# Four images on one core: when the second layer's rows T and the next image's second rows xx are loaded

## The chip, the core and the metric

The kernel runs on one core of one Trainium2 chip. The metric is the device time of one execution in microseconds; several executions are made and the median is given. One execution is also taken with the hardware profiler, and every duration of a single instruction comes from that one.

## What is computed

The input x has 4 images of 32 channels and 128 x 128 points. In layer 0 each image is rearranged into 128 rows (32 channels by 2 x 2 points) of 4096 columns:

```python
q = xs.reshape(B, C * R * R, hw)
energy = jnp.einsum('bci,bcj->bij', q, q)      # 4096 x 4096
d = jnp.sqrt(jnp.diagonal(energy, axis1=1, axis2=2))
attn = jax.nn.softmax(energy / (d[:, :, None] * d[:, None, :]), axis=-1)
out = gamma * jnp.einsum('bcj,bij->bci', q, attn) + xs
```

Layer 1 takes the result as 4096 tokens of 128 numbers an image:

```python
t = t + _L1_attn_ref(_ln_t(t), Wk, Wq, Wv)      # linear attention, 8 heads
t = t + _L1_ffn_ref(_ln_t(t), router_w, router_b, expert_w, expert_b)   # 2 of 8 experts
```

## The kernel before

**Layer 0, `attend`.** The 4096 columns of an image are 8 chunks of 512. Row i of the work goes over the chunks jc = 0 to i; so a row has i blocks off the diagonal and one on it, and the last row, i = 7, is the longest. For each quarter of a block PE makes the energies (pe, L556), ACT their exponentials (pr, L559), and PE multiplies them into the row's sum (po, L440). The energies are symmetric. Each block off the diagonal is therefore used a second time, transposed: DVE transposes it in pieces of 32 x 32 into F (L369); SP writes F to DRAM, 1 MB (blocks, L483, in `move`); when that has landed SP brings it back in another order by four DMAs of 256 KB (G, L491, in `bring`); and 57 units of the planned clock later PE multiplies G into the sum of the other chunk (pg, L375). Diagonal blocks go the same way in smaller form (L498, L506, L396). Three buffers are there for F and three for G.

**Layer 1.** `layer1` makes all that comes after layer 0 for an image. Its `all_parts` is the steady stream: it starts near the end of the image's own `attend` and runs on beside the next image's. T holds the image's rows, 2 MB in SBUF in a single buffer (tag "T" of `big1`); `input_rows` loads it from x by 4 groups of 4 DMAs of 128 KB (image 0: 8 groups with half as much each; the DMAs are those of L279, tile T). `close_rows` adds the result of layer 0 to T and normalises it, `attention_rows` adds the attention, stores T to DRAM (t2, L897) and normalises it a second time, and `sorted_experts` handles the experts. It scatters the normalised rows into DRAM sorted by expert (POOL, L989), SP loads the sorted rows (L1013), PE multiplies them (pys), SP stores the results (ys, L1035), POOL gathers two rows for each token (yb, L1114), DVE combines them into acc, which ACT's queue has fetched from t2 (L1090), and SP puts acc into the output (L1096, `put`). The tokens are handled in two halves. Image 3 has nobody beside it, and its experts are worked out without sorting in `last_parts`.

**`prep`.** `prep(b, kc, st)` loads a quarter of image b's rows (xx, 4 DMAs of 128 KB, also L279), transposes them on PE (ptq, L313), sums their squares on DVE, takes the power -1/2 on POOL (L164), scales, and transposes again (ptn, L346). Of the next image the quarters 0 and 1 are made during the current one, 2 and 3 at the beginning of its own.

**The order.** The order of every engine's instructions is written out by hand; each engine and each DMA queue takes its own in that order. A clock counts work of PE, and t is the percent of an image that is done. Each stream of instructions is a generator. The streams in `timed` have a begin, an end and a count of steps: such a stream moves a step whenever t has passed its share of the stretch. T and xx are such streams. The steady stream moves a step every 10 units of the clock. So a DMA's place in SP's queue is set by t, and what is issued before it on SP goes first. In images 1 to 3, by this plan, the last normalisation that reads the previous image's T is issued at t = 32.1; its scatters at 34.4 to 60; the loads of sorted rows at 50.5 to 79; the gathers at 71 to 95; the puts from 79 on; the first `close_rows` of the image at 94.

The places the change touches are the planner's lines L1327 to L1332.

Of the kernel before, what the change touches and what calls it, by code (L numbers as in the profile page):

```python
# [22 lines left out]
def kernel(  # L23
# [45 lines left out]
    B, C, H, W = x.shape  # L69
# [66 lines left out]
    def setup_sorting():  # L136
        def iota(dst, pattern, part=0):
            nc.gpsimd.iota(
                dst, pattern=pattern, base=0, channel_multiplier=part, allow_small_or_imprecise_dtypes=True
            )  # L140

        iota(rank_below, [[1, P]], part=-1)
        nc.vector.tensor_scalar(rank_below, rank_below, 0.0, None, ALU.is_gt)
        iota(upto, [[1, E], [-1, E]])
        nc.vector.tensor_scalar(upto, upto, 0.0, None, ALU.is_ge)
        iota(tiles_of[:, 0, :], [[P, HR]])
        iota(tile_no[:, :, 0], [[1, NT]])
        yield
        yield

        rows = x.rearrange("b c h w -> (b c h) w")
        step = NT * P // 8
        for g in range(16):
            inst = nc.scalar.dma_start(xs[g // 8][ts(g % 8, step), :], rows[ts(g, step), :])
            xs_made[g // 8].append(inst.ins)
            yield
            yield
# [5 lines left out]
    def pow_neg_half(dst, src):  # L163
        pinned(nc.gpsimd.tensor_tensor(dst, src, neg_half.to_broadcast(list(src.shape)), ALU.pow))  # L164
# [13 lines left out]
    def idle(n):  # L178
        for _ in range(2 * n):
            yield  # L180

    def keep_running(n, pool=None, tag=None):

        bank = psum_t("spare") if pool is None else pool.tile([P, CH], F32, tag=tag, name="spare")
        for _ in range(n):
            nc.tensor.transpose(bank[:, :P], ident, ident)
# [4 lines left out]
    def hold(name, evict, alloc=psum_t):  # L191


        while len(held) >= banks[0]:
            held[0]()
        bank = alloc(name)

        def done():
            if done in held:
                held.remove(done)  # L200
                evict(bank)

        held.append(done)
        return bank, done
# [69 lines left out]
    def load_tokens(dst, b, k0, nk, queues=(nc.sync, nc.sync)):  # L274
        src = tokens(x, b)
        for s in range(2):
            for r1 in range(2):
                p0 = s * 64 + r1 * 32
                queues[r1].dma_start(dst[p0 : p0 + 32], src[s, r1, :, k0 : k0 + nk, :])  # L279


    def prep(b, kc, st):

        if b == 0:
            if kc == 0:
                st["all"] = big1.tile([P, 4, 8, HW2, 2], F32, tag="T", name="xx_0")
            xx = st["all"][:, kc]
        else:
            xx = xin.tile([P, 8, HW2, 2], F32, tag="xx", name=f"xx_{b}_{kc}")
        first = b == 0 and kc == 0  # L290
        load_tokens(
            xx.rearrange("p k w r -> p k (w r)"), b, 8 * kc, 8, (nc.sync, nc.scalar if first else nc.sync)
        )
        qT = qpool.tile([P, 2, NJ, P], F32, tag="qT", name=f"qT_{b}_{kc}")
        st.setdefault("qT", {})[2 * kc] = qT[:, 0]
        st["qT"][2 * kc + 1] = qT[:, 1]
        yield
        yield
        yield from idle(2 if b else 1)

        def load_half(g, pt):
            nc.vector.tensor_copy(
                qT[:, :, 2 * g : 2 * g + 2, :].rearrange("p s j (r c) -> p (j r) s c", c=64),
                pt.rearrange("p (m s c) -> p m s c", s=2, c=64),
            )

        for g in range(2):
            yield
            pt, done = hold(f"ptq_{b}_{kc}_{g}", partial(load_half, g))
            for jj in range(2):  # L310
                for r2 in range(2):
                    k = 4 * g + 2 * jj
                    nc.tensor.transpose(  # L313
                        pt[:, ts(2 * jj + r2, P)], xx[:, k : k + 2, :, r2].rearrange("p k w -> p (k w)"), ident
                    )
            yield
            done()
        yield
        yield
        ss = stat.tile([P, 2 * NJ], F32, tag="ss", name=f"ss_{b}_{kc}")  # L320
        rn = stat.tile([P, 2 * NJ, 1], F32, tag="rn", name=f"rn_{b}_{kc}")
        for s in range(2):
            sq = work.tile([P, NJ, P], F32, tag="qs", name=f"sq_{b}_{kc}_{s}", bufs=2)
            nc.vector.tensor_tensor(sq, qT[:, s], qT[:, s], ALU.mult)
            nc.vector.tensor_reduce(ss[:, ts(s, NJ)], sq, AX.X, ALU.add)  # L325
            if first:
                pow_neg_half(rn[:, ts(s, NJ), 0], ss[:, ts(s, NJ)])
            elif s == 1:
                pow_neg_half(rn[:, :, 0], ss)
            yield  # L330
            yield
        yield from idle(1)
        if first:
            keep_running(22, ps_g, "pg")
        scaled = []
        for s in range(2):
            qs = work.tile([P, NJ, P], F32, tag="qs", name=f"qs_{b}_{kc}_{s}", bufs=2)
            nc.vector.tensor_tensor(qs, qT[:, s], rn[:, ts(s, NJ)].to_broadcast([P, NJ, P]), ALU.mult)
            scaled.append(qs)
        for s, qs in enumerate(scaled):  # L340
            yield
            qn = npool.tile([P, CH], F32, tag="qn", name=f"qn_{b}_{2 * kc + s}")
            st.setdefault("qn", {})[2 * kc + s] = qn
            pt, done = hold(f"ptn_{b}_{kc}_{s}", lambda p, qn=qn: nc.scalar.activation(qn, p, AF.Copy))  # L344
            for j in range(NJ):
                nc.tensor.transpose(pt[:, ts(j, P)], qs[:, j, :], ident)  # L346
            yield
            done()
        yield
        yield  # L350
# [242 lines left out]
    def input_rows(b, st):  # L593
        st["T"] = T = big1.tile([P, KT, D], F32, tag="T", name=f"T_{b}")
        nk = 4 if b == 0 else 8
        for k in range(0, KT, nk):
            load_tokens(T[:, k : k + nk, :], b, k, nk)
            yield
            yield
            yield from idle(1)  # L600
# [718 lines left out]
    timed = [(first, 0, 1, 4)]  # L1319
    for b in range(B):  # L1320

        if b == 0:
            for kc, begin, end in ((1, 0, 5), (2, 6, 20), (3, 25, 45)):
                timed.append((prep(0, kc, states[0]), begin, end, 12))
            timed.append((setup_weights(), 46, 58, 9))
            timed.append((setup_sorting(), 58, 98, 17))
        if b + 1 < B:  # L1327
            nxt = states[b + 1]
            timed.append((prep(b + 1, 0, nxt), 65, 82, 13))
            timed.append((prep(b + 1, 1, nxt), 83, 99, 13))  # L1330
        begin, end, count = (52, 94, 17) if b == 0 else (55, 75, 9) if b == B - 1 else (82, 99, 9)
        timed.append((input_rows(b, states[b]), begin, end, count))  # L1332
        done = [0] * len(timed)
        start = clock[0]
        closing = None
        for half, _ in enumerate(chain(attend(b, states[b]), finish() if b == B - 1 else ())):
            if half % 2 == 0:
                t = 100 * (clock[0] - start) / UNITS
                moved = []
                if closing is None and t > 84:  # L1340
                    closing = layer1(b, states[b])
                    steady.append([closing.first_parts() if b == B - 1 else closing.all_parts(), clock[0]])
                for n, (steps, begin, end, count) in enumerate(timed):
                    if t >= begin and done[n] * (end - begin) < (t - begin) * count:
                        moved.append(steps)
                        done[n] += 1
                for stream in steady:
                    if clock[0] >= stream[1]:
                        stream[1] = clock[0] + PACE
                        moved.append(stream[0])  # L1350
            for steps in moved:
                next(steps, None)
        for steps, *_ in timed:
            for _ in steps:
                pass
        timed = []
        if b + 1 < B:
            timed.append((prep(b + 1, 2, nxt), 2, 20, 13))
            timed.append((prep(b + 1, 3, nxt), 30, 50, 13))
# [43 lines left out]
```

## Time and profile before

| what | us |
|---|---|
| median of three runs | 1753.12 (1751.01 to 1756.18) |
| the profiled execution, whole | 1738.44 |
| its span | 1736.7 |
| PE busy in the span | 1660.1 |
| DVE, ACT, POOL busy | 940.4, 928.7, 513.3 |
| DMA of the hardware queue of SP | 314.91 MB, 64.4% of the 16 engines' span |

The span is the time from the first instruction to the last, and it is a little shorter than the execution. PE busy divided by the span is PE's share. A wait is read from an engine's timeline: the brackets behind an instruction give the idle time before it and what ended it. In the page's DMA row each digit is the busy share of the 16 DMA engines in a fortieth of the span. The granted clock of PE has a mean of 0.988.

### The profile page before, as it was taken

What the parts mean: (1) busy time and instruction counts of PE and PEld (TensorE: products, weight loads), DVE (VectorE), ACT (ScalarE), POOL (GpSimd) and SP (SyncE); (2) the same over time, 40 slices, a digit from 0 to 9 for tenths busy, and PEclk for the clock granted to TensorE, in tenths of its full rate; (3) what the DMA queues carried; (4) which work ended last, traced back from release to release, by engine and by line L of the source; (5) the groups of instructions that cost most, each with busy time, mean ns of one, the idle gap of its engine ahead of it and who ended that gap; (6) DMA issues with size and microseconds to landing.
All of it is one profiled execution on the core that took longest, in us unless ns stands there. A gap on an engine that the chain in (4) does not pass through costs nothing. (4 is left out here: it accounts for less than half of the span.)

```text
span 1736.7 us, 21220 instructions
## 1 busy us (share of the span) xinstructions
PE 1660.1 (96%) x5458; PEld 879.4 (51%) x5458; DVE 940.4 (54%) x2443; ACT 928.7 (53%) x2893; POOL 513.3 (30%) x553
## 2 busy tenths in 40 slices
PE   8999999999999999889999999979999999999887
PEld 5444444455644555445554455534555455544633
DVE  4433334467585335567477334546748533455687
ACT  3555445466565555446565555535556555445376
POOL 1000000011037506540015722552102760464166
PEclk9999999999999999999999999999999999999999
DMA  4675877876567899987567889998656889995001
GB/s 132 199 203 169 213 209 231 249 216 182 178 189 246 254 269 255 254 234 203 163 186 218 251 260 264 259 244 213 200 157 193 244 257 261 272 269 137 1 13 37
DMA packets 240681, 355.25 MB, mean 205 GB/s; under 512 B 27312, under 2 KB 155312, under 8 KB 226480
## 3 DMA queue, kind: packets, MB, share of 16 engines
q1 hardware_dynamic: 220048, 314.91, 64.4%
q0 software_dynamic: 12288, 25.19, 5.0%
q10 hardware_dynamic: 8224, 13.77, 2.9%
q8 instruction: 46, 0.75, 0.2%
q14 instruction: 75, 0.61, 0.1%
HBM read 183.64 MB, written 173.15 MB: 205 GB/s over the span
## 5 line engine op out<-in xcount | busy, mean ns | idle before, releaser
L559 ACT ACTIVATE pr<-pe 128x512 f32<-128x512 f32 (+1 forms) x576 | 322.4, 560 | 544.1 <-PE pe L556 504.7
L440 PE MATMUL po<-pr,qT 128*128 128x512 f32 (+3 forms) x1152 | 552.0, 561 | 3.9 <-ACT o L445 3.9
L375 PE MATMUL pg<-G,qT 128*128 128x512 f32 x880 | 455.5, 599 | 37.0 <-DMA G<-blocks 28.9
L556 PE MATMUL pe<-qn,qn 128*128 128x512 f32 x896 | 463.1, 599 | 1.9 <-ACT pr L559 1.6
L369 DVE STREAM_TRANSPOSE F<-pr 128x512 f32<-128x512 f32 x440 | 306.1, 702 | 150.1 <-ACT pr L559 146.8
L440 PEld LDWEIGHTS po<-pr,qT 128*128 128x128 f32 x1152 | 216.6, 191 | 251.7 <-issue 221.4
L380 ACT ACTIVATE junk<-G 128x512 bf16<-128x512 f32 x440 | 273.0, 620 | 37.6 <-DMA G<-blocks 35.3
L375 PEld LDWEIGHTS pg<-G,qT 128*128 128x128 f32 x880 | 166.9, 192 | 238.1 <-issue 190.1
L1114 POOL DMA_INDIRECT yb<-ys,place x192 | 186.2, 970 | 276.1 <-DMA xn<-xs 102.7
L989 POOL DMA_INDIRECT xs<-xn,place x192 | 185.6, 966 | 118.6 <-ACT pr L559 56.2
L556 PEld LDWEIGHTS pe<-qn,qn 128*128 128x128 f32 x896 | 155.7, 192 | 113.9 <-issue 102.4
L385 DVE TENSOR_TENSOR o<-o,pg 128x512 f32<-128x512 f32 x110 | 75.5, 686 | 212.5 <-PE pg L375 212.0
L164 POOL TENSOR_TENSOR rn<-ss,neg_half 128x8 f32<-128x8 f32 (+1 forms) x17 | 27.7, 1634 | 395.4 <-DVE ss L325 395.4
L559 ACT ACTIVATION_READ_ACCUMULATOR pr<-pe 128x1 f32 x576 | 111.9, 194 | 0.0
L1023 ACT ACTIVATE xn<-pys 128x256 f32<-128x256 f32 (+1 forms) x120 | 44.9, 377 | 104.8 <-PE pys L1056 104.7
L164 POOL TENSOR_TENSOR rsf<-dm_f,neg_half 128x8 f32<-128x8 f32 (+1 forms) x15 | 26.2, 1746 | 235.1 <-DVE sv_f L636 235.1
L1049 PEld LDWEIGHTS pys<-ew_sb,xn 128*128 128x128 f32 x468 | 68.4, 191 | 47.6 <-issue 44.9
L556 PE MATMUL pe<-qn 128*128 128x512 f32 (+3 forms) x256 | 90.7, 437 | 0.7 <-ACT qn L344 0.7
L380 ACT ACTIVATION_READ_ACCUMULATOR junk<-G 128x1 f32 x440 | 84.3, 192 | 0.0
L1032 DVE COPY result<-pys 128x256 f32<-128x256 f32 (+1 forms) x60 | 24.6, 411 | 100.8 <-ACT xn L1023 73.3
L1083 DVE SCALAR_TENSOR_TENSOR acc<-yb,weight,acc 128x128 f32<-128x128 f32 x192 | 65.6, 342 | 21.3 <-DMA yb<-ys,place 13.1
L1049 PE MATMUL pys<-ew_sb,xn 128*128 x468 | 71.2, 275 | 4.1 <-DVE result L1032 4.1
(189 smaller groups left out, 1574.9 us busy)
## 6 DMA issues: line engine op xcount, KB each, us to landing
blocks<-F SPq DMA_DIRECT2D x108, 1024.0 KB
G<-blocks SPq DMA_DIRECT2D x432, 256.0 KB
xn<-xs SPq DMA_DIRECT2D x114, 128.0 KB
below<-F SPq DMA_DIRECT2D x31, 384.0 KB
G<-below SPq DMA_DIRECT2D x124, 96.0 KB
out_dram<-acc SPq DMA_DIRECT2D x128, 64.0 KB
xx<-in_x_dram SPq DMA_DIRECT2D x62, 128.0 KB
ys<-xn SPq DMA_DIRECT2D x60, 128.0 KB
```

The lines of the kernel that those rows point to most:

```text
L164: pinned(nc.gpsimd.tensor_tensor(dst, src, neg_half.to_broadcast(list(src.shape)), ALU.pow))
L369: f()
L375: nc.tensor.matmul(pg.rearrange("p (a f) -> p a f", a=4), st["qT"][i][:, ib, :], G[:, :, ib], start=(ib == 0), stop=(ib == NJ - 1),)
L380: nc.scalar.activation(junk, G[:, :, ib], AF.Copy, accum_out=st["sums"][:, NJ * i + ib, jc : jc + 1])
L385: nc.vector.tensor_tensor(o, o, pg.rearrange("p (a j c) -> p a j c", a=4, c=S), ALU.add)
L440: nc.tensor.matmul(row["po"][:, lo:hi], qT[blk // NJ][:, blk % NJ, :], w, start=start, stop=(row["left"] == 0))
L556: nc.tensor.matmul(pe[:, c0:], qn[jc][:, ts(j, P)], qn[i][:, c0:], start=True, stop=True)
L559: nc.scalar.activation(pr[:, c0:], pe[:, c0:], AF.Exp, accum_out=sums[:, t, i : i + 1]).ins
L989: inst = nc.gpsimd.indirect_dma_start(xs[h], offset(place[:, i, k : k + 1]), xn[:, k, :], None)
L1049: nc.tensor.matmul(p[:, 2 * P + j * D : 2 * P + j * D + D], bufs[4 + g % 2][:, j, :], weights[:, bass.ds(begins[2 * (g % 2) + j], D)], sta ...
L1083: nc.vector.scalar_tensor_tensor(a[:, k % 4, :], yb[k // 4][:, i, k % 4, :], weight[:, i, k, :], a[:, k % 4, :], ALU.mult, ALU.add)
L1114: inst = nc.gpsimd.indirect_dma_start(yb[k // 4][:, i, k % 4, :], None, ys, offset(place[:, i, k : k + 1]))
```

## The change

```diff
         if b + 1 < B:
             nxt = states[b + 1]
             timed.append((prep(b + 1, 0, nxt), 65, 82, 13))
-            timed.append((prep(b + 1, 1, nxt), 83, 99, 13))
-        begin, end, count = (52, 94, 17) if b == 0 else (55, 75, 9) if b == B - 1 else (82, 99, 9)
+            timed.append((prep(b + 1, 1, nxt), 87, 99, 13))
+        begin, end, count = (52, 94, 17) if b == 0 else (36, 47, 9)
         timed.append((input_rows(b, states[b]), begin, end, count))
```

T of images 1 and 2 was planned into 82 to 99 percent of the image and T of image 3 into 55 to 75; all three are now planned into 36 to 47. Image 0's stays at 52 to 94. In images 0, 1 and 2 the second quarter of the next image, `prep(b + 1, 1)`, was planned into 83 to 99 percent and now goes into 87 to 99, with the same number of steps. No instruction is added or removed.

## The prediction

> **What bounds the kernel now.** I read four views of the profile: the page, the busy time by stage (windows), the timeline of PE with what ended its idle time, and the timeline of SP's queue. The page says that TensorE is the bound nearly everywhere and that the DMA engines fill up toward the end of an image.
>
> ```profile
> PE 1660.1 (96%) x5458; PEld 879.4 (51%) x5458; DVE 940.4 (54%) x2443; ACT 928.7 (53%) x2893; POOL 513.3 (30%) x553
> ...
> DMA  4675877876567899987567889998656889995001
> ```
>
> PE is busy 1660.1 of 1736.7 us, so 76.6 us are idle, and only idle or half-clocked PE time can be won. The DMA row rises to 9s three times: near the ends of images 1, 2 and 3. (Counting exponentials of L559, 144 to an image, the images begin at 15, 370, 782 and 1199 us.) The stages around the change:
>
> ```profile
> core 0: us, PE busy (x) PEld busy (x) DVE busy (x) ACT busy (x) POOL busy (x), PEclk, DMA share, GB/s
> ...
> 510.00:545.00 35.00, 34.82 (x100) 17.00 (x99) 25.60 (x70) 17.30 (x55) 24.44 (x26) 1.00 0.75 228
> ...
> 700.00:760.00 60.00, 48.30 (x114) 21.65 (x113) 30.34 (x65) 21.37 (x67) 31.38 (x33) 0.91 0.95 247
> ...
> 1120.00:1200.00 80.00, 65.90 (x177) 31.41 (x176) 46.26 (x112) 32.51 (x101) 35.09 (x35) 0.94 0.95 235
> ...
> 1405.00:1480.00 75.00, 75.00 (x296) 43.63 (x294) 25.86 (x52) 39.72 (x122) 16.51 (x18) 1.00 0.92 248
> ```
>
> Where T is loaded now in images 1 and 2 (700 to 760 and 1120 to 1200), DMA is at 95% and PE loses 11.7 and 14.1 us, at a lowered clock besides. Where T will be loaded (510 to 545 in image 1) DMA is at 75% and PE loses 0.18 us. PE's timeline names what it waits for in the first of the bad stages:
>
> ```profile
> 717.21 2.04 PE L375 MATMUL pg<-G,qT 128*128 128x512 f32 x2 [3.89 <-DMA G<-blocks]
> ...
> 732.16 1.10 PE L375 MATMUL pg<-G,qT 128*128 128x512 f32 x2 [1.85 <-DVE F L369]
> ...
> 748.65 2.05 PE L375 MATMUL pg<-G,qT 128*128 128x512 f32 x2 [5.96 <-DMA G<-blocks]
> ```
>
> The product of a transposed block (pg) needs its four G transfers. G lands late, so SP's queue is the place to look:
>
> ```profile
> 703.11 2.07 SPq L279 DMA_DIRECT2D T<-in_x_dram  x4
> 705.27 0.39 SPq L1035 DMA_DIRECT2D ys<-result  x1
> 705.84 7.41 SPq L491 DMA_DIRECT2D G<-blocks  x4
> 713.29 1.91 SPq L279 DMA_DIRECT2D xx<-in_x_dram  x4
> 715.30 0.39 SPq L483 DMA_DIRECT2D blocks<-F  x1
> 715.79 3.83 SPq L1096 DMA_DIRECT2D out_dram<-acc  x4
> 723.26 1.74 SPq L491 DMA_DIRECT2D G<-blocks  x4
> 725.04 2.55 SPq L279 DMA_DIRECT2D T<-in_x_dram  x4
> 731.65 0.34 SPq L483 DMA_DIRECT2D blocks<-F  x1
> ```
>
> One queue carries everything in program order: the block to DRAM, its return as G, T, xx, the results. G's four issues take 7.41 us instead of 1.74: the trace's semaphore records show eight DMA semaphores used in turn by SP and ACT, and an issue waits until the DMA eight places earlier has landed (the fourth G began at 712.94; the holder, an acc<-t issued on ACT's queue at 706.42, landed at 712.92). So each T group, four DMAs of 128 KB, costs bytes, half of the eight places, and SP's time.
>
> **What the Trainium skill says.** "DMA: Bandwidth & Descriptors", section "Issuing engines are not separate DMA queues": DMAs of all issuing engines share the same 16 DMA engines and interleave; the ACT-issued acc<-t above, 6.5 us under way between SP's transfers, agrees. Same page, "Anatomy of one DMA": waits on semaphores happen on the issuing sequencer, not in the DMA engines; the 7.41 us agree. "TensorE: Matmul & The Clock Gate", section "HAM oscillation": a throttled stretch costs half its length. The trace's clock records have half-clock stretches of 3.41 us from 717.07 and 6.83 us from 747.79, and the pair of L375 took 2.04 us there against 1.10 at 732.16.
>
> **The change, part by part.** Positions are percent of an image's planned clock (UNITS), found by stepping the generators by hand.
>
> (1) T of images 1 and 2 leaves 82.65, 86.22, 90.05 and 93.88 (16 DMAs, 2 MB each image). Price of a group: the DMA packet records give 4096 packets of 512 B at a mean 32 ns over 16 engines, 8.2 us per T, 2.05 per group; the landings of the first group in image 1 lie 0.65 us apart, 2.6. On the queue it is more. From one G to the next in row 7 of image 1 (SP starts 705.84, 723.26, 738.77, 752.04, 767.4, 778.3, 788.4) SP takes 17.4, 15.5, 13.3, 15.4, 10.9, 10.1 us; the 15.5, 13.3 and 15.4 hold a group and a put each, the 10.9 a put alone. A group costs 14.7 - 10.9 = 3.8 us there; the first costs about 2.3. Sum 2.3 + 3 x 3.8 = 13.7 us of queue. Image 2 has 14.8, 15.3, 14.1, 16.3, 11.5, 10.4: the same picture, 4.3 a group.
>
> What PE can win: image 1 idles 3.89 + 1.85 + 5.96 + 1.10 (at 794.8) = 12.8, and runs about 9.4 us at half clock while busy, 4.7: 17.5 in all. Image 2: 2.44 + 3.64 + 5.96 + 2.06 + 0.36 = 14.5, plus 4.4: 18.9. Walking image 1 with the groups gone: G(7,0) lands about 2.5 us earlier (3.89 becomes 1.4), G(7,1) about 7 (its gap closes), G(7,2) about 8 to 9, G(7,3) to G(7,6) 10 to 14. PE without stalls takes about 11 us from pg to pg, as much as the queue then needs. I get 13 us at row 7's end, less part (2).
>
> (2) xx of prep(b+1, 1) moves from 83.42 to 87.24 (image 0) or 87.76 (images 1 and 2), past the issue of a block write and, in images 1 and 2, past G(7,1): 2.6 us of transfer leave in front of one G and stand in front of the next. Its transposes on PE now follow 2.6 to 3.1% behind the load instead of 3.8%: 11 us in place of 15. xx needs 7 us from issue to landing and SP is 5 us behind PE there, so the ptq transposes, queued on PE ahead of everything later, wait. Before, xx landed at 720.1 and PE took it at 722.34, after a stall; that was the whole slack. I take 3 us of wait (bounds 0 and 5) in each of images 0 to 2. In 1 and 2 it partly replaces G(7,2)'s gap; I subtract it whole: 13 - 3 = 10 each. In image 0 it meets the 2.29 us wait for G<-blocks at 339.47, which goes (2.6 us less ahead of it); net +0.5 (bounds -1.5 and +2). The rest of prep is squeezed from 16% to 11% of an image and ends by 98.1 as before; rn of POOL stands behind gathers that end at 95.4. Nothing for it, at worst 1 us.
>
> (3) T of image 3 leaves 55.1 to 68.4. No PE stall lies there (75.00 of 75.00 busy), but the lag it leaves ends in 3.37 us at 1484.58 (pys behind a result buffer whose store is late), then 1.77 and 2.17 for G, and 1.7 of clock: 9.0. DMA stays at 97% to 1560 without T, so I take the first with its clock, 5 us in all (bounds 1 and 9).
>
> (4) T arrives at 36.5, 38.7, 41.6 and 43.9 in all three images. The previous T's last readers are at 32.14 (normalise) and 31.38 (store), 16 us earlier: no wait. Behind the groups on SP stand G(4,2), G(4,3), the diagonal and G(5,0). SP issued G(4,3) until 531.64, it landed at 537.1, PE came at 543.24: 6.1 us to spare, the least of the stage in image 1. Price of a group: below 0.5 if it fills DMA's idle quarter while SP waits for a block to land, 2.6 if not. I take 1.2: three groups 3.6, inside 6.1. Image 3's old groups are the nearest row: four of them at 92% DMA, with no stall. Cover gone, each us over 6.1 is a us of PE. POOL's scatters slow beside them, with nobody waiting before 50.5%.
>
> Sum: image 0 +0.5, images 1 and 2 -10 and -10.5, image 3 -5: **-25 us**. The span goes from 1736.7 to 1711.7; the profiled execution took 1738.44 (1.74 around the span), the median of the runs shown is 1753.12, 14.7 above it. I subtract the same 25 from it: **1728**.
>
> **The rivals.**
> Small gain: the bytes alone count, 2.05 to 2.6 per group up to G(7,2), and the ptq waits and a half-clock stretch stay: -5, -5, -3, about 1740. For it: SP's eight places stay full with puts and blocks. Against: the 10.9 us spacing as soon as no group is in it.
> Large gain: every stall named goes, 17.5 + 18.9 + 9.0 less a few us, about -41: 1712. Against: the ptq wait, and the DMA share of image 3.
> No change: the DMA chain of images 1 and 2 is late already by 700, and xx moved into the worst stretch gives back what T leaves: 1753. Against: 7 to 10 us to spare for G until 657, and 4.2 still at 691.
> Slower: in the new place a group delays the G behind it by p us, as SP waits in order for a block's landing. PE stalls by 3p - 6.1 an image, and 1.7 for the clock. At p = 5 that is 10.6 in each of three images and eats the whole 25 plus 7; it decides from p = 4.2, and at 5.4 the sum is +10, where I put the case: 1763. For it: the queue price of 3.8 in the full stage. Against: a quarter of the DMA time is free.
>
> **How the numbers follow.** Forecast 0.50; small gain 0.20; large gain 0.14; no change 0.07; slower 0.09. A measurement of this kernel tells about 0.3% (5 us) from no change. Faster 0.50 + 0.20 + 0.14 = 0.84, same 0.07, slower 0.09. The range 1708 to 1748 takes in the first three with the bounds of their costs and leaves out the last two, 0.16.
>
> **What would show it.** Right: 700 to 760 with PE near 55 of 60 or more, no 6.83 us half-clock stretch, G-to-G spacing near 11 us in row 7, 510 to 545 at a DMA share over 0.85 with PE still over 34.5 busy, ptq waiting for xx by some us. Wrong: idle at L375 before 570 in image 1, or row 7's spacing still 13 to 15 us with no T in it.

## The result and the profile after

| kernel | median us (lowest to highest) | ratio to before, 95% interval |
|---|---|---|
| before | 1752.07 (1749.98 to 1756.18) | |
| after | 1731.59 (1728.70 to 1733.49) | 0.9881 [0.9853, 0.9909] |

The change saves 20.5 us. The forecast was 1728, so 25. The profiled execution of after took 1730.18 us, with a span of 1728.4.

From the page of after, the engines' busy time and the DMA row:

```profile
PE 1656.8 (96%) x5458; PEld 876.9 (51%) x5458; DVE 939.3 (54%) x2443; ACT 925.8 (54%) x2893; POOL 511.8 (30%) x553
...
DMA  4775778876569899996568979998656988995001
```

PE does the same 5458 instructions. In the DMA row a 9 has come up in the slices 12, 22 and 31 (counted from 0; from 518, 951 and 1339 us), which is T's new place; near the image ends the row stays at 8 and 9. The stages of the prediction, in the windows of after:

```profile
core 0: us, PE busy (x) PEld busy (x) DVE busy (x) ACT busy (x) POOL busy (x), PEclk, DMA share, GB/s
510.00:545.00 35.00, 34.81 (x97) 16.87 (x97) 25.60 (x76) 18.16 (x60) 24.17 (x24) 1.00 0.96 259
700.00:760.00 60.00, 56.26 (x146) 26.37 (x145) 34.03 (x75) 26.14 (x83) 33.98 (x35) 0.94 0.92 256
1120.00:1200.00 80.00, 74.30 (x211) 36.13 (x210) 53.17 (x138) 38.77 (x123) 38.87 (x39) 0.98 0.90 250
1405.00:1480.00 75.00, 73.67 (x291) 43.06 (x292) 28.95 (x59) 40.37 (x125) 15.23 (x16) 1.00 0.88 253
```

In T's new place (510 to 545) the DMA share rose from 0.75 to 0.96, and PE is busy for 34.81 us where it was for 34.82. In the old place (700 to 760) PE went from 48.30 to 56.26 of 60 us. DMA is hardly less busy there (0.95 to 0.92): other transfers moved up. This window favours this profile, in which row 7 begins 8 us later than before (its first G is issued at 713.54, before at 705.84). In the profile of the same kernel from the first group of experiments row 7 begins at 704.57, and the window has

```profile
700.00:760.00 60.00, 53.44 (x135) 24.09 (x134) 38.57 (x91) 24.85 (x78) 35.44 (x36) 0.97 0.97 265
```

against 48.87 busy in before on that chip. PE's timeline of after names what is left of the waits of image 1 (the number in front is the start of the instruction, so a wait lies ahead of it; "issue" means that the profile shows nothing that was waited for):

```profile
583.34 1.22 PE L1049 MATMUL pys<-ew_sb,xn 128*128 x4 [3.74 <-ACT xn L1023]
...
736.38 2.04 PE L375 MATMUL pg<-G,qT 128*128 128x512 f32 x2 [2.70 <-DMA G<-blocks]
...
762.22 1.10 PE L375 MATMUL pg<-G,qT 128*128 128x512 f32 x2 [0.56 <-DMA G<-blocks]
765.58 0.66 PE L346 MATMUL ptn<-ident,qs 128*128 128x128 f32 x4 [2.27 <-issue]
```

The waits at L375 fell from 3.89 + 1.85 + 5.96 + 1.10 to 2.70 + 0.56. Two lines are new. The wait of ptn (2.27 us, prep's second transposes) was not in the prediction. The wait of pys ahead of 583.34 was not either; 3.36 us ahead of 999.91 and 3.44 ahead of 1406.33 are its like in images 2 and 3. The section on the chips below comes back to it. SP's timeline of after through row 7:

```profile
713.54 1.85 SPq L491 DMA_DIRECT2D G<-blocks  x4
...
715.97 10.93 SPq L1096 DMA_DIRECT2D out_dram<-acc  x4
727.06 2.81 SPq L491 DMA_DIRECT2D G<-blocks  x4
...
731.31 2.62 SPq L279 DMA_DIRECT2D xx<-in_x_dram  x4
735.53 4.01 SPq L1096 DMA_DIRECT2D out_dram<-acc  x4
740.39 2.38 SPq L491 DMA_DIRECT2D G<-blocks  x4
...
743.37 10.13 SPq L1096 DMA_DIRECT2D out_dram<-acc  x4
753.67 1.75 SPq L491 DMA_DIRECT2D G<-blocks  x4
```

From one G to the next SP takes 13.5, 13.3, 13.3, 11.1, 11.1 and 9.6 us (before: 17.4, 15.5, 13.3, 15.4, 10.9, 10.1). No T is in the queue now, yet three of the distances are 13 us and not the 11 that was forecast: in two of them a put's four issues take 10.93 and 10.13 us, as those of T's last group did before (10.10 from 755.25); in the third stand xx and a put.

### The profile page after: what moved, and what is told of

Same layout as the page of the kernel before. It is cut to its first block, busy times and chain, and to the rows that moved or that the text cites. A ratio compares the mean times of both kernels' runs of the same rounds, so it can differ in the third digit from the quotient of the medians.

```text
span 1728.4 us, 21211 instructions
## 1 busy us (share of the span) xinstructions
PE 1656.8 (96%) x5458; PEld 876.9 (51%) x5458; DVE 939.3 (54%) x2443; ACT 925.8 (54%) x2893; POOL 511.8 (30%) x553
## 5 line engine op out<-in xcount | busy, mean ns | idle before, releaser
L375 PE MATMUL pg<-G,qT 128*128 128x512 f32 x880 | 453.4, 597 | 14.1 <-DMA G<-blocks 8.7
L375 PEld LDWEIGHTS pg<-G,qT 128*128 128x128 f32 x880 | 167.5, 192 | 214.0 <-issue 187.0
L1023 ACT ACTIVATE xn<-pys 128x256 f32<-128x256 f32 (+1 forms) x120 | 45.0, 377 | 118.3 <-PE pys L1056 67.7
L1049 PEld LDWEIGHTS pys<-ew_sb,xn 128*128 128x128 f32 x468 | 68.5, 192 | 56.3 <-issue 39.0
L164 POOL TENSOR_TENSOR rsa<-dm_a,neg_half 128x8 f32<-128x8 f32 x16 | 26.4, 1650 | 219.3 <-DVE sv_a L636 219.0
L1049 PE MATMUL pys<-ew_sb,xn 128*128 x468 | 72.1, 277 | 11.1 <-ACT xn L1023 11.0
```

The lines of the kernel that those rows point to most:

```text
L375: nc.tensor.matmul(pg.rearrange("p (a f) -> p a f", a=4), st["qT"][i][:, ib, :], G[:, :, ib], start=(ib == 0), stop=(ib == NJ - 1),)
L1023: nc.scalar.activation(bufs[4 + g % 2][:, :n], p[:, : n * P].rearrange("p (j t) -> p j t", t=P), AF.Copy)
L1049: nc.tensor.matmul(p[:, 2 * P + j * D : 2 * P + j * D + D], bufs[4 + g % 2][:, j, :], weights[:, bass.ds(begins[2 * (g % 2) + j], D)], sta ...
```

## The experiments

Twelve runs, in three groups of four; each group ran on one chip, beside runs of before on the same chip (their median is given with the group). Differences in us are those of the medians of one group; between groups the ratios are compared. The diffs are against the changed kernel; where the text says "prep at 83", the line of e1 that puts it there belongs to the edit too and is not shown again.

**First group (before: 1739.80 us).** The change taken apart.

`e1_t_only`: T moved, prep where it was.

```diff
-            timed.append((prep(b + 1, 1, nxt), 87, 99, 13))
+            timed.append((prep(b + 1, 1, nxt), 83, 99, 13))
```

> T of images 1 to 3 moved as in the change, the next image's second rows left at 83. Theory (T's four groups are what makes G late in row 7): at least the whole gain of the change, 20 to 25 us (ratio about 0.987), image 0 unchanged against before, and PE's idle time at L375 in row 7 of images 1 and 2 under half of what it was. Rival (the second rows' shift past G(7,1) is what helps): 10 us or less (ratio 0.995 or above).

Measured: 1711.45 us, 0.9839 [0.9818, 0.9860], 28.4 us saved.

`e2_prep_only`: prep moved, T where it was.

```diff
-        begin, end, count = (52, 94, 17) if b == 0 else (36, 47, 9)
+        begin, end, count = (52, 94, 17) if b == 0 else (55, 75, 9) if b == B - 1 else (82, 99, 9)
```

> Only the next image's second rows moved from 83 to 87, T left in its old places. Theory: no change within 5 us (ratio 0.997 to 1.003), image 0 ends about 2 us later with a wait of ptq for xx. Rival: 10 us faster.

Measured: 1736.82 us, 0.9980 [0.9966, 0.9994].

`e3_after_again` and `e4_before_again`: the two kernels unchanged.

> The change once more, to see whether the three new stalls of about 3.5 us at the first products of the sorted rows (L1049, near 54% of images 1 to 3) belong to the kernel or to one profiled execution. If they belong to it: again three stalls of 3 to 4 us at L1049. If not: fewer, or elsewhere. Time about 0.988 of before.

Measured: 1716.99 us, 0.9871 [0.9851, 0.9891], 22.8 us saved; none of the three waits of pys is in its profile.

> The kernel before once more, since its profiled execution was 14.7 us shorter than the median of its timed ones. Theory: an execution near 1752 us shows the same stalls at L375 in row 7 of images 1 and 2, only longer, by 10 to 15 us in all. Rival: the difference lies elsewhere (a lower clock, the end of the kernel, image 0).

Measured: one execution, 1735.89 us, with much the same waits as the profile of before (35.2 us at L375 against 37.0). It was not an execution near 1752 us, so it does not show where such a one loses its time.

T's move alone is worth more than the whole change: the later prep costs 5.5 us beside it (1716.99 - 1711.45). The profiles show where. PE's groups of instructions in the kernel before on this chip (`e4`; the last columns are the idle time ahead of the group and what ended it):

```profile
L375 PE MATMUL pg<-G,qT 128*128 128x512 f32 x880 | 455.1, 599 | 35.2 <-DMA G<-blocks 30.6 <-DMA out_dram<-acc 1.8 <-DVE acc L1083 1.5
L1049 PE MATMUL pys<-ew_sb,xn 128*128 x468 | 71.6, 276 | 3.7 <-DVE result L1032 3.7
L313 PE MATMUL ptq<-ident,xx 128*128 128x128 f32 x128 | 20.9, 289 | 5.9 <-DMA xx<-in_x_dram 5.9
L346 PE MATMUL ptn<-ident,qs 128*128 128x128 f32 x128 | 19.4, 274 | 0.7 <-DVE qs L338 0.7
```

with T alone moved:

```profile
L375 PE MATMUL pg<-G,qT 128*128 128x512 f32 x880 | 453.7, 597 | 19.5 <-DMA G<-blocks 12.2 <-DVE acc L1083 3.5 <-issue 2.8
L1049 PE MATMUL pys<-ew_sb,xn 128*128 x468 | 71.1, 275 | 0.0
L313 PE MATMUL ptq<-ident,xx 128*128 128x128 f32 x128 | 20.9, 290 | 6.4 <-DMA xx<-in_x_dram 6.4
L346 PE MATMUL ptn<-ident,qs 128*128 128x128 f32 x128 | 19.4, 274 | 1.3 <-DVE qs L338 1.3
```

and with the whole change:

```profile
L375 PE MATMUL pg<-G,qT 128*128 128x512 f32 x880 | 451.3, 594 | 15.3 <-DMA G<-blocks 7.0 <-issue 3.7 <-DVE acc L1083 3.1
L1049 PE MATMUL pys<-ew_sb,xn 128*128 x468 | 71.1, 275 | 0.9 <-DVE result L1032 0.9
L313 PE MATMUL ptq<-ident,xx 128*128 128x128 f32 x128 | 21.2, 291 | 10.1 <-DMA xx<-in_x_dram 10.1
L346 PE MATMUL ptn<-ident,qs 128*128 128x128 f32 x128 | 19.5, 275 | 5.4 <-DVE qs L338 5.4
```

T's move takes 15.7 us from L375 and all 3.7 of pys, 18.3 us with the little that ptq and ptn wait more. The clock records of the two profiles have 27.3 and 13.7 us of half clock before 1600 us, so the clock gives at most half of the difference, 6.8 us. Together that is 25.1 of the 25.5 us between the spans (1734.0 and 1708.5). (5.9 us of ptq's wait are the kernel's start and belong to all of them.) The later prep takes 4.2 more from L375, and gives back 3.7 at ptq and 4.1 at ptn. With T still in row 7 the same trade is larger and comes out a little ahead: in `e2` PE waits 5.25 us for ptq and 3.09 for ptn in image 1, and L375's 11.1 of before in that image are 4.2. The group xx is one more group in front of G, as T's are.

**Second group (before: 1740.07 us).** Image 3, the new place, the time of prep, another place.

`e5_t12_only`: prep at 83, T of image 3 left where it was.

```diff
-        begin, end, count = (52, 94, 17) if b == 0 else (36, 47, 9)
+        begin, end, count = (52, 94, 17) if b == 0 else (55, 75, 9) if b == B - 1 else (36, 47, 9)
```

> T of images 1 and 2 at 36 to 47, T of image 3 left at 55 to 75, prep at 83 as before. The kernel with T of all three moved stood at 0.9839. Theory: T of image 3 is worth 4 to 5 us of its own (the stall of pys at L1049 and what follows it), so this one stands near 0.9865, and the 3.4 us stall at L1049 in image 3 is there again. Rival: what image 3 won came from entering it with less lag behind, so T of image 3 is worth nothing there: 0.984 and no stall at L1049.

Measured: 1719.35 us, 0.9873 [0.9848, 0.9899]. The wait at L1049 is back, in PE's timeline of this run:

```profile
1461.01 0.77 PE L1049 MATMUL pys<-ew_sb,xn 128*128 x4 [3.49 <-DVE result L1032]
```

So T of image 3 is worth (0.9873 - 0.9839) of 1740, 5.9 us, of its own, though the two intervals overlap; the wait's place shows it better than the times.

`e6_t_twice`: prep at 83, and T's groups loaded a second time in the new place.

```diff
             load_tokens(T[:, k : k + nk, :], b, k, nk)
+            if b > 0 and k > 0:
+                load_tokens(T[:, k - nk : k, :], b, k - nk, nk)
             yield
```

> T moved, prep at 83, and from the second group on each step of T loads the group before it once more (12 more DMAs of 128 KB, 1.5 MB, in each of images 1 to 3; the same values). Theory of the prediction: a group costs 1.2 us of the queue in the new place, three more are 3.6, inside the 4.8 to 6 us that G(4,3) has to spare: PE does not wait in row 4, within 0.002 of the 0.9839 with T once. Rival (the prediction's slower case): a group costs 2.6 us or more there; three more are 7.8 or more and PE waits 3 to 6 us for G in row 4 of each image: 0.989 to 0.994.

Measured: 1716.21 us, 0.9855 [0.9832, 0.9878]. SP's timeline in the new place:

```profile
520.57 9.55 SPq L279 DMA_DIRECT2D T<-in_x_dram  x8
530.76 2.05 SPq L491 DMA_DIRECT2D G<-blocks  x4
...
533.76 6.94 SPq L279 DMA_DIRECT2D T<-in_x_dram  x8
...
543.98 5.52 SPq L279 DMA_DIRECT2D T<-in_x_dram  x8
549.61 2.45 SPq L491 DMA_DIRECT2D G<-blocks  x4
```

PE has no wait at L375 in row 4 of any image. G(4,2) is the return of row 4's block jc = 2. From the semaphores' records, the time that G(4,2), G(4,3), G(5,0) and G(5,1) of image 1 had landed before PE came is, in us:

| profile | G(4,2) | G(4,3) | G(5,0) | G(5,1) |
|---|---|---|---|---|
| before, shown ahead of the prediction | 7.1 | 6.1 | 8.5 | 8.4 |
| before, first group | 7.4 | 6.2 | 9.0 | 9.0 |
| T once, prep at 83, first group | 6.3 | 5.9 | 7.7 | 7.4 |
| the change, first group | 5.3 | 4.9 | 5.8 | 5.0 |
| T twice, prep at 83, this group | 6.1 | 3.4 | 1.9 | 1.9 |

Against before on the same chip, the four groups took up to 1.6 us with T once, 0.4 a group, and up to 4.0 in the changed kernel, 1.0 a group (one profile each). The three further ones took up to 5.8, 1.9 a group, as the DMA share in 510 to 545 went from 0.96 to 1.01; that compares two chips. The new place carries T once cheaply, and twice just so.

`e7_prep79`: T moved, prep four percent earlier than before.

```diff
-            timed.append((prep(b + 1, 1, nxt), 87, 99, 13))
+            timed.append((prep(b + 1, 1, nxt), 79, 99, 13))
```

> T moved, prep(b+1, 1) begun at 79 in place of 83 (87 in the change). Theory: xx standing in front of G(7,0) and G(7,1) is what is left of row 7's stalls at L375 (3.6 us at 726 and at 1129 with prep at 83), so taking it out of row 7 wins 1 to 3 us in each of images 1 and 2: 0.981 to 0.983, no ptq or ptn wait over 1 us. Rival: with T gone the queue of row 7 is filled by puts and blocks and xx only moves to an equally full place: 0.9839 within 0.001, the same stalls at L375.

Measured: 1710.37 us, 0.9824 [0.9802, 0.9847]. The interval overlaps widely with that of prep at 83 (0.9818 to 0.9860), so which of the two is faster is not settled. In the profile the wait at L375 of 3.62 us in row 7 of image 1 (T alone, first group) has become 1.94, and that in image 2 3.16 from 3.53. But 1.97 and 1.74 us come up at L375 just behind the ends of the two images, and its whole idle time is 19.1 us against 19.5. So the expected gain from taking xx out of row 7 is not shown.

`e8_t60`: T moved to another place outside row 7, prep at 83.

```diff
-        begin, end, count = (52, 94, 17) if b == 0 else (36, 47, 9)
+        begin, end, count = (52, 94, 17) if b == 0 else (60, 73, 9)
```

> T of images 1 to 3 at 60 to 73 in place of 36 to 47, prep at 83. Theory: what counts is that T is out of row 7; G has 7 to 10 us to spare up to 73 percent, four groups of 1.2 to 2.6 us fit, but leave the queue some us later at the beginning of row 7: 0.985 to 0.987. Rival: the stretch beside the scatters is needed because the DMA engines have a free quarter there and none later; at 60 to 73 beside the loads of sorted rows and xx each group costs the 3.8 us of row 7: 0.990 or more, with L375 waiting in row 6.

Measured: 1736.82 us, 0.9981 [0.9969, 0.9993]. The rival's number, but not its mechanism: row 7 is as good as with T at 36 (L375 waits 3.9 us in image 1), and L375 does not wait in row 6. The loss is at pys, in PE's timeline of this run:

```profile
654.60 1.19 PE L1049 MATMUL pys<-ew_sb,xn 128*128 x4 [6.70 <-DVE result L1032]
```

and the tile of the results shows who holds it up, from 640 to 656 us:

```profile
its engine sat idle before it (us, times) until:
  DMA ys<-result: 12.0, 3
...
who waited for it (us, times):
  DVE result L1032: 9.6, 2
  PE pys L1049: 6.7, 1
```

SP's stores of results stand behind T's groups (one, issued at 647.87 right behind T's last group, landed at 654.07), the result buffers come free late, DVE cannot copy out of pys (its copy starts at 654.16), and PE stops; the same with 7.54 us in image 2 and 3.05 in image 3, with a half-clock stretch of 6.83 us at each of the first two. This is what T of image 3 did in before ahead of 1484.58. What matters is not only that T leaves row 7: from 50 to 79 percent the sorted experts' loads and stores need the queue as well, and 36 to 47 lies before their first.

**Third group (before: 1755.80 us).** What the later prep costs, the price of a group in row 7, and the order of the two versions again.

`e9_xx83`: T moved, xx loaded at 83, the rest of prep where the change has it.

```diff
+    def once(steps):
+        next(steps)
+        yield
...
-            timed.append((prep(b + 1, 1, nxt), 87, 99, 13))
+            second = prep(b + 1, 1, nxt)
+            timed.append((once(second), 83, 84, 1))
+            timed.append((second, 87.92, 99, 12))
```

> T moved; only xx of prep(b+1, 1) is loaded at 83, as before, and the rest of prep keeps the squeezed places that it has in the change (88 to 99). Prep at 83 with T moved stood at 0.9839, the change at 0.9871. Theory: what the later prep costs is the late load; ptq waits for xx by 1 to 1.6 us and what follows it (ptn, 3.07 us) is late because of that. Here both waits are gone and the ratio is 0.984 within 0.001. Rival: it is the squeeze; the ptq waits go, the ptn wait of 3 us in image 1 stays since scaling and power come too close in front of it: 0.986 to 0.987.

Measured: 1732.59 us, 0.9863 [0.9837, 0.9889]. The ratio is the rival's, though its interval takes in the 0.984 of the theory as well; the waits decide for the rival. ptq does not wait in row 7 any more; ptn does, in PE's timeline of this run in image 1:

```profile
736.87 2.05 PE L375 MATMUL pg<-G,qT 128*128 128x512 f32 x2 [3.99 <-DMA G<-blocks]
...
768.13 0.66 PE L346 MATMUL ptn<-ident,qs 128*128 128x128 f32 x4 [2.87 <-DVE F L369]
```

and 2.90 us in image 2. What stands in front of it is seen in DVE's timeline of the changed kernel (first group), where ptn waited 3.07 us until 755.05:

```profile
746.87 2.78 DVE L709 TENSOR_TENSOR df<-o,pbd 64x512 f32<-64x512 f32 x4
...
750.93 1.22 DVE L731 TENSOR_TENSOR T<-T,df 128x1024 f32<-128x1024 f32 x1
...
753.70 0.69 DVE L385 TENSOR_TENSOR o<-o,pg 128x512 f32<-128x512 f32 x1
754.30 1.29 DVE L338 TENSOR_TENSOR qs<-qT,rn 128x512 f32<-128x512 f32 x2
```

POOL had rn ready at 748.13 (1.67 us from 746.46). The scaling qs then stood on DVE behind the first `close_rows` of the image (L709, L731) and a normalisation, 6 us. With prep at 83 the scaling comes ahead of L731, at 749.95, and ptn runs at 750.96 without a wait. So the last stretch of the planned clock, in which prep is squeezed from 16% to 11%, is also where `close_rows` begins.

`e10_t_half`: prep at 83, T's last two groups of images 1 and 2 back in row 7.

```diff
-        begin, end, count = (52, 94, 17) if b == 0 else (36, 47, 9)
-        timed.append((input_rows(b, states[b]), begin, end, count))
+        if b in (1, 2):
+            timed.append((input_rows(b, states[b], 0, KT // 2), 36, 41, 5))
+            timed.append((input_rows(b, states[b], KT // 2, KT), 90, 99, 5))
+        else:
+            begin, end, count = (52, 94, 17) if b == 0 else (36, 47, 9)
+            timed.append((input_rows(b, states[b]), begin, end, count))
```

> T moved, prep at 83, but in images 1 and 2 the last two of T's four groups are back at 90 and 93.6 percent, in row 7. Theory of the prediction: a group costs 3.8 us of the queue in row 7 wherever it stands there, and G has nothing to spare at 745 to 770 (0.37 us of wait at 753.65 with T moved): two groups give back about 7 us in each of the two images, 0.992, with L375 waiting between 745 and 775. Rival 1: bytes alone, 2.05 to 2.6 a group: 0.989. Rival 2: only the two groups in front of G(7,1) and G(7,2) hurt, since the lag starts there; the later ones fit beside work: 0.984 to 0.986.

Measured: 1741.24 us, 0.9909 [0.9883, 0.9936]; 13.4 us above the T-only kernel beside it, 3.3 us for each of the four groups put back. L375 waits 2.91, 1.83 and 2.29 us ahead of 745.58, 758.83 and 773.67, where it was expected; the T-only kernel has only the first of these (2.92 us ahead of 743.89). But the interval holds both 0.992 and the 0.989 of the bytes alone, so the times do not tell the two apart. The queue shows 4.5 us for the two groups of image 1: G to G, the two distances with a group took 12.9 and 16.0 us, and without it on the same chip 12.5 and 11.8. In image 2 it is 3.6 (14.2 and 13.1 against 12.0 and 11.7). That is 2.0 us of queue a group, near the 2.05 that the prediction had for the bytes alone; the 3.3 us of the kernel's time are more, half clock included (`e10` has 13.7 us of it from 700 to 1200, the T-only kernel 6.8).

`e11_t_again` and `e12_after_third`: T alone moved, and the change, once more.

> The kernel with T moved and prep at 83 once more, beside the other runs of this group: 0.984 within 0.002 if the order of the earlier runs (it ahead of the change) is the kernel's and not that day's.

> The changed kernel once more beside it: 0.987 within 0.002, 3 to 8 us above the kernel with T alone moved, with ptq waiting for xx by 1 to 2 us in image 1 or 2. Rival: the difference of 5 us between the two was scatter, and here they stand within 2 us.

Measured: 1727.86 us, 0.9837 [0.9813, 0.9862], and 1732.41 us, 0.9865 [0.9838, 0.9892]. The order is the same on another chip, 4.6 us apart, though here the intervals overlap. ptq waited 1.90, 3.08 and 2.19 us in images 0, 1 and 2 of the changed kernel, and ptn at most 0.92 in row 7: in this profile the cost lies at the load, in that of `e9` at the squeezed rest.

**The version ahead of both.** T moved and prep left at 83: 0.9839 and 0.9837 on two chips, where the change has 0.9871 and 0.9865.

## Why the prediction was right, point by point

The sum was -25; the changed kernel measured -20.5, -22.8 and -23.4 (1755.80 - 1732.41) in three sets of runs. By image, the executions profiled on the first group's chip, counted by the exponentials (image 0 from the start, image 3 to the end):

| us | before | T alone | change | predicted difference | measured difference |
|---|---|---|---|---|---|
| image 0 | 367.6 | 369.4 | 368.8 | +0.5 | +1.2 |
| image 1 | 412.3 | 403.5 | 404.4 | -10 | -7.9 |
| image 2 | 415.9 | 402.8 | 406.1 | -10.5 | -9.8 |
| image 3 | 538.2 | 532.9 | 532.9 | -5 | -5.3 |

T alone changes nothing in image 0, yet image 0 is 1.8 us longer there; so a difference of a row is known to about 2 us only, and image 0's +0.5 is neither borne out nor refuted.

(1) **T out of row 7: right, with one of its terms too large.** By the prediction's own terms T alone is -31.5 (the 25, with 0.5 + 3 + 3 of part 2 left out); it measured -28.4 and -27.9; by the table, images 1 and 2 gained 8.8 and 13.1 of the 13 and 13.5 us taken. The term that was too large is the queue's price of a group, 3.8 us in image 1 and 4.3 in image 2. (By the rule used for image 1 the distances of image 2 give 15.2 - 11.5 = 3.7; 4.3 comes out only if the last distance, which has no put, is averaged in.) Put back, a group took 2.0 us of the queue; taken away, the three distances that held a group fell from 44.8 to 35.7 us on the first group's chip, 3.0 a group.

The rule took the later distances, 10.9 us, for what a row 7 without T would have everywhere. That is not so: the distances of image 1 are 16.8 (with xx), 12.1, 11.6, 12.0, 10.9 and 10.6 with T alone moved, and 11.8, 13.7 (with xx), 12.3, 11.2, 10.9 and 9.9 in the change on the same chip. One reason is in SP's waits between 700 and 770 us, of before:

```profile
SPq L279 <- DMA acc<-t: 10.1, 2, 6.3
SPq L491 <- DMA blocks<-F: 6.7, 2, 3.5
SPq L491 <- DMA acc<-t: 5.8, 1, 5.8
SPq L483 <- DMA acc<-t: 4.0, 1, 4.0
...
SPq L1096 <- DMA acc<-t: 1.4, 1, 1.4
```

and with T alone moved:

```profile
SPq L491 <- DMA blocks<-F: 11.5, 4, 4.9
SPq L1096 <- DMA acc<-t: 7.9, 2, 6.9
SPq L491 <- DMA acc<-t: 6.2, 2, 5.5
SPq L483 <- DMA acc<-t: 5.1, 1, 5.1
```

(The columns are the line that waits, what ended its waits, their sum, number and the longest.) SP waited 21.3 us for acc<-t to land (20.9 in the before of the first group), waits 19.2 with T alone moved, and 17.2 in the change on the same chip. The prediction knew the mechanism, eight semaphores used in turn, an issue waiting for the DMA eight places earlier, and met it with an acc<-t. But it charged to T what T's issues merely stood in: the waits of L279 fell to the puts (L1096) when T had gone. With T alone moved the waits for a block's own landing, blocks<-F, even grew. The 3.62 us that PE still waits ahead of 729.89 with T alone moved can be followed back to such a place: the write of the block was held 5.09 us, until an acc<-t landed at 715.53; the block landed at 721.13, its G was issued from 721.20 and landed at 729.75. Whether PE would wait less with acc<-t elsewhere was not tried.

(2) **The later prep: right in size, incomplete in its parts.** Predicted cost 6.5 us, measured 5.5 and 4.6 beside T's move. ptq waits for xx, 1.0 to 3.1 us an image in the first and third group, against 3 (bounds 0 and 5); in the profile of after it waits 1.92 us in image 0 and hardly at all in images 1 and 2. But "Nothing for it, at worst 1 us" for the squeezed rest of prep was wrong: ptn waits 3.07 us in image 1 of the first group and 2.27 and 2.52 in images 1 and 2 of the profile of after. The prediction looked at POOL's queue (rn behind gathers), and the wait is on DVE's, behind `close_rows`. That the sum of this part came out near is therefore partly luck: ptq waited less than was taken, and ptn, taken at nothing, made up for it (the two together are 2.3 to 4.1 us in images 1 and 2 of the three profiles, against the 3 of ptq alone). With the load back at 83 the cost stayed (0.9863 against 0.9865), so the squeezed rest alone seems to be enough for it; a late load without the squeeze was not tried.

(3) **Image 3: right.** -5 by its stall at L1049 and the clock behind it, -5.3 measured (the stall in before on this chip is 3.58 us, with 3.41 of half clock); putting its T back brings the stall back, 3.49 us.

(4) **The new place: right.** 1.2 us a group were taken between bounds of 0.5 and 2.6; it was 0.4 with T alone and 1.0 in the changed kernel, where T fills the idle quarter of the DMA time, and about 1.9 for more groups when that quarter was full. The rival of the slower side needed 4.2.

**The other rivals.** Small gain (1740) and large gain (1712) both fall outside what was measured; T's move alone, 28 us below before, does not reach the large one's 41 either. No change and slower are refuted by the times, and by the windows of row 7 and of 510 to 545.

**The signs.** The DMA share of 0.96 in 510 to 545 with PE at 34.81: as forecast. PE near 55 of 60 in 700 to 760: 56.26 in after, but 53.44 and 52.02 in the first and third group, where the window holds more of row 7. ptq waiting by some us: in image 0 of after, in all three images of the other two profiles. "No 6.83 us half-clock stretch" was wrong: after has one from 735.71, behind the wait of 2.70 us. It is gone in the other two profiles of the same kernel, in which row 7 of image 1 has one of 3.41. G spacing near 11: three of six distances, and the other three are 13.3 to 13.5. Spacing of 13 to 15 us with no T in it was named as a sign of being wrong; it came in part, and what it points at is the price of a group in (1), not the place of T.

## The chips

The prediction subtracted its 25 us from a median that was 14.7 above the profiled execution, without a reason for the distance. The runs suggest one: the kernel before took 1740 us beside the first two groups and 1756 beside the third, each on one chip, and the ratio of the same change is 0.9871 and 0.9865 there. The three waits of pys in the profile of after go the same way. They are in all four profiles of the third group, 1.0 to 3.8 us long (3.40 us ahead of 577.18 in image 1 of T alone, for instance), and at that place in none of the first two groups. The profile of before, then, looks like a chip of the first kind and that of after like one of the second, which would explain why their spans differ by 8.3 us only. Each chip was used in one group alone, so that it is the chip and not the hour is not shown. That before has these waits on the slower chip was not profiled, and what causes them stays open: in T alone of the third group PE stands at pys, ACT's copy of xn (L1023) begins after 5.11 us of idle time, and semaphore records are missing around it.

## What to carry to other kernels

A load with a long lead goes where the DMA time has a free share and nobody on the same queue is short of buffers; leaving the worst place is not enough, since at 60 percent nearly the whole gain was lost at another wait (0.9981). When a transfer that stood in a wait is removed, ask for whom the wait was: if the holder of the place stays, the next issue inherits it. And a stream that is squeezed at the end of a stage is checked on every engine that it passes, in the order of that engine's queue, for the first work of the next stage may be there already.

## What the runs showed of the hardware

The same kernel took 1740 us on two chips and 1756 on a third, 0.9% more, while the ratio of two kernels was the same within 0.1%.

The half-clock stretches of PE came as 3.41 or 6.83 us in every profile before the kernels' ends. The length of the wait does not tell whether one follows: 2.03 us ahead of 725.91 (the change, first group) brought 3.41, 2.70 ahead of 736.38 (after) brought 6.83, and 3.64 ahead of 1145.63 (before) brought none. At the same place in row 7, 3.89 us (before) brought 3.41 and 3.88 us (before, first group, ahead of 715.13) brought 6.83. In each of the 14 profiles the beginnings of all its stretches lie whole multiples of 3.413 us apart: in before, from 717.07 to 747.79 it is 9, and from there to 1160.80 it is 121. So it seems to matter where a wait lies against this grid and not only how long it is; that was not tried.
